# Two layers on one core: reordering dense products, transposes and sums between the hooks of an attention and two feed-forward stages

## The chip, the cores and the metric

The kernel runs on one core of a Trainium2 chip. The metric is the time of one execution in microseconds (us) of device time; lower is better. TensorE is written PE in the profile (PEld is its weight load), VectorE is DVE, ScalarE is ACT, GpSimd is POOL, SyncE is SP.

## The reference

Two layers act on x of 2 x 1024 x 512 in float32. Each takes a layer norm and adds an attention-like branch and a feed-forward branch:

```python
xn = _layernorm(x)
x = x + L0_attn(xn, ...) + L0_ffn(xn, W1, W2, W3)    # scan of rank 8 + small MLP; silu(x W1) * (x W3), Hadamard, W2
xn = _layernorm(x)
x = x + L1_attn(xn, W_qkv, ...) + L1_ffn(xn, w_gate, w_up, w_down)
# L1_attn: 16 heads of 32, causal softmax over 1024 keys, output projection
# L1_ffn: h = silu(xn w_gate) * (xn w_up); keep 2 of every 4 hidden values; h w_down
```

## The kernel before, in words

All matrix products are float32. There are three stages, one after the other.

**Stage a (layer 0).** The hidden width of 2048 is cut into 16 units of `gate_up` (8 for each half of the rows). One unit forms its two products by a scheme with seven half-size products: in order `pa` from `w1`, `pc` from `s[0]`, `pa` from `s[1]`, `pb` (the "other half"), `pa` from `s[2]`, `pa` from `w2`, `pc` from `s[3]`. Each takes TensorE about 3.44 us. `pa`, `pb` and `pc` are pairs of PSUM banks. Between them ScalarE copies `pa` to `e[0..2]` (lines 214, 222, 228) and VectorE adds `pb` or `pc` to an `e` (lines 210, 232, 242); a later product into the same banks waits for that reader. With `split=True`, `pb` is formed in two parts, one before and one after the product from `s[2]`.

At seven places of a unit, `hook(0)` to `hook(6)`, other work is issued. A list holds it: `put0(unit, place, ...)` in stage a, `put1` in stage c; place 8 of unit 2 is hook 1 of unit 3. What is put there:

- The down projection of one pair of units (`down_by_seven`): seven products `m = 0..6` for each of two halves, 1.72 us of TensorE each (line 305). `hidden_first` (lines 273, 274) and `hidden_last` (lines 280, 281) are four VectorE subtractions and additions that make their inputs; product 1 needs the first of `hidden_last`. In stage a `hidden_last` overwrites an input of product 0, so it also waits for that one. `add_u2` (line 323) adds a partial result on GpSimd.
- The low-rank branch, and `prepare_last`, which makes a few small sums with TensorE: four transposes (line 498), three groups of four tiny products (lines 503, 508, 512). The third group needs ScalarE's copy of the transposes.

**Stage b (attention).** There are 8 units `u` (batch and a group of four heads), and 12 steps `(u, j, kt)` for each, 96 in all, numbered `n`. A step issues `weights` (lines 1139, 1145: scores of transposed keys, exp on ScalarE at line 1156, mask at lines 1161 or 1165), then `gather` of the step before (line 1185: weights times values into bank 0; line 1192: sums of the weights), then `maxima` for 13 steps later (line 1082, then VectorE lines 1089, 1090), then one or more **dense parts**: half of a projection (`project`, `values`, `project_out`, line 1030), 1.91 us from start to start of what follows. Dense parts are taken from the list `rest` with entries (earliest step, due step, parts): the ready one with the nearest due step goes first, one part a step, more where the planner (`late`) finds them behind. `put_after(n, ...)` places work right after `gather`; `put(n, ...)` places it at the end of a step. Two such pieces share step 12u+7 and step 12u+15: `total` (line 1204: weight sums to `w`, copied by ScalarE into the single buffer `inv`, then four reciprocals and a product in `divide`) and `shift_rows` (line 1120: transposes of the negated maxima to `px`, copied by VectorE at line 1124).

PSUM in this stage: three pairs of banks, `wide0..2`, are handed out in turn to everything wide: `weights` takes two, `maxima` two, `total` one, `shift_rows` one. Bank 0 holds the output of `gather`. A dense piece takes bank 1 if `alone` is None, and banks 0 and 1 in turn otherwise.

`idle_vector(u, j, kt)` is true from the step on in which no `maxima` are left (`12u + 4j + kt + 13 >= 96`): then masks are made on VectorE, and with `j = 1` the sums of line 1192 too; before that both are GpSimd's.

**Stage c (layer 1 feed-forward)** has 16 units of the same `gate_up`, the same down projection, and between them `sparsify`: one ScalarE and eleven VectorE instructions (lines 1449 to 1464) that keep two of four, issued by `some_steps`. The last pair of units ends in a list `tail`, with whole-row products at line 1508.

Within each stage TensorE, VectorE, ScalarE and GpSimd execute in the order in which the program issues; DMAs on SP are free of it, and so is what comes after the 96 steps.

Of the kernel before, what the change touches and what calls it, by code (L numbers as in the profile page):

```python
# [35 lines left out]
def two_layers(ctx: ExitStack, tc: tile.TileContext, t: dict, out: bass.AP):  # L36
# [315 lines left out]
    with tc.tile_pool(name="a", bufs=1) as a:  # L352
# [131 lines left out]
        def prepare():  # L484
            nc.gpsimd.tensor_mul(gd, gd, factors["dskip"])
            nc.gpsimd.tensor_mul(wo_aug, wo_aug, factors["Wo_by"])
            wa = wp[:, :, R : 2 * R]
            b_wide, wo_t = row("b_wide"), row("wo_t")
            b_wide, wo_t = (v.rearrange("p (k c) -> p k c", c=P) for v in (b_wide, wo_t))
            nc.gpsimd.tensor_copy(b_wide, bcol.unsqueeze(2).to_broadcast([P, KC, P]))  # L490
            ones = a.tile([P, P], F32, name="ones_a")
            nc.gpsimd.memset(ones, 1.0)
            put0(1, 1, prepare_last, wa, b_wide, wo_t, ones)

        def prepare_last(wa, b_wide, wo_t, ones):
            pw, pc = two_banks("prep")
            for k in range(KC):
                nc.tensor.transpose(
                    pw[:, k * P : (k + 1) * P], wo_aug[:, k * P : (k + 1) * P], ident
                )  # L500
            nc.scalar.copy(wo_t.rearrange("p k c -> p (k c)"), pw)
            for k in range(KC):
                nc.tensor.matmul(
                    pc[:, : 2 * R], b_wide[:, k, :], w_io[:, k, :],
                    start=(k == 0), stop=(k == KC - 1),
                )
            for k in range(KC):
                nc.tensor.matmul(
                    pc[:, 2 * R : 3 * R], ones, wa[:, k, :], start=(k == 0), stop=(k == KC - 1)
                )  # L510
            for k in range(KC):
                nc.tensor.matmul(
                    pc[:, 3 * R : 4 * R], wo_t[:, k, :], wa[:, k, :],
                    start=(k == 0), stop=(k == KC - 1),
                )
            nc.vector.tensor_add(c_io, b_io, pc[:, : 2 * R])
            nc.vector.tensor_copy(cs_a, pc[:, 2 * R : 3 * R])
            nc.vector.tensor_copy(woa[:32, :], pc[:32, 3 * R : 4 * R])
# [259 lines left out]
        for n in range(NU - 1):  # L778
            u = 2 * n + 2
            places = [range(7), range(7, 14)]  # L780
            if n == 0:
                places = [(7, 8, 8, 9, 9, 10, 10), (11, 12, 12, 13, 13, 14, 14)]
            elif n == 1:
                places = [range(1, 8), (8, 9, 10, 11, 12, 13, 13)]
            for half, at in enumerate(places):
                put0(u, at[0] - half, hidden_first, n, half)
                for f, *args in products_of(n, half):
                    if f == down:
                        place = at[args[2]]
                    put0(u, place + (f != down), f, *args)  # L790
                    if f == down and args[2] == 0:
                        put0(u, place, hidden_last, n, half)

            for m, (k, f) in enumerate(((1, 1), (3, 1), (6, 1))):
                at = places[1][k] + f
                put0(u, at, down_weights, n + 1, m)
# [142 lines left out]
    with tc.tile_pool(name="b", bufs=1, reuse_waits="tile") as b:  # L939
# [234 lines left out]
        def gather(u, j, kt, s, pts):  # L1174

            bb, hg = units[u]
            if kt == 0:
                held[u, j] = ps_bank(f"o_{u}_{j}", 0)
                sums_of[u, j] = pts
            po = held[u, j]  # L1180
            last = kt == 4 * j + 3
            v = vals[bb, kt // NJ, kt % NJ][:, hg * P : (hg + 1) * P]
            for h in range(4):
                rows = slice(h * HD, (h + 1) * HD)
                nc.tensor.matmul(  # L1185
                    po[rows, s:], v[:, rows], pts[h // 2][:, h % 2, s:],
                    start=(kt == 0), stop=last, tile_position=(0, h * HD),
                )
            if kt:
                eng = nc.vector if j and idle_vector(u, j, kt) else nc.gpsimd  # L1190
                for acc, pt in zip(sums_of[u, j], pts):
                    eng.tensor_add(acc[:, :, s:], acc[:, :, s:], pt[:, :, s:])  # L1192
            if last:
                att[u, j] = b.tile([P, 512], F32, tag="att", name=f"att_{u}_{j}", bufs=12)
                nc.scalar.copy(att[u, j], po)
# [58 lines left out]
        def put_after(n, *what):  # L1254

            after.setdefault(n, []).append(what)

        for u in range(len(units)):

            for half in range(2):  # L1260
                n = per * u - ahead + (3, 11)[half]
                if half:
                    put(n + 1, larger, u)
                for m in range(3):
                    put_mid(n + 2 + m, shift_part, u, half, m)
                put_after(n + 5, shift_rows, u, half)
            if u:
                lo = per * (u - 2) if u > 1 else -ahead
                for x in range(4):
                    rest.append((lo, per * u - ahead - 1, project(u, x // 2, x % 2)))  # L1270
            if u > 1:
                put(per * (u - 2) - 1, load_qk, units[u][1])
            for j in range(2):
                n = per * u + 8 * j + 7
                if n < len(second):
                    put_after(n, total, u, j)
                    for q in range(4):
                        put(n + q * 2 // 3, divide, u, j, q)
                else:
                    put(len(second) + 2, total, u, j)  # L1280
        for x in range(4):
            rest.append((-ahead, x, values(0, 0, x)))
            rest.append((-ahead, 7 + x, values(0, 1, x)))
# [15 lines left out]
        for m in range(QT):  # L1299


            lo, hi = (per * 5 + 6, per * 6 + 3) if m < NJ else (per * 6, per * 8 - 6)
            if m > NJ:
                lo = per * 8 - (17, 14, 2)[m - NJ - 1]
                hi = lo + 1
            rest.append((lo, hi, project_out(m)))

        def do_first(n):
            u, qt, c = first[n]
# [32 lines left out]
        for x in range(4):  # L1342
            for f, *args in project(0, x // 2, x % 2):
                f(*args)
        behind, alone = None, None
        start = mark()
        for n in range(-ahead, len(second)):
            now = weights(*second[n]) if n >= 0 else None
            for f, *args in middle.pop(n, ()):
                f(*args)  # L1350
            if behind is not None:
                gather(*behind)
            behind = now
            for f, *args in after.pop(n, ()):
                f(*args)
            if n < 0:
                one_part(n)
            if n + ahead < len(first):
                do_first(n + ahead)
            if n >= 0 or n % 2:  # L1360
                one_part(n)
            while late(n) and one_part(n):
                pass
            what_is_fixed(n)
# [1 line left out]
        gather(*behind)  # L1366
        alone = 0
        n = len(second)
        for m in range(QT, QT + NJ):
            rest.append((n, n + 9, project_out(m)))  # L1370
        first_tt, *make = combine_x(sums, xt1[0], xt1[1], "c0")
        for m, f in enumerate(make):
            put(n + 5 + m, f)
# [12 lines left out]
    with tc.tile_pool(name="c", bufs=1, reuse_waits="tile") as c_:  # L1386
# [131 lines left out]
        for n in range(groups - 1):  # L1518

            end = n == groups - 2  # L1520
            u = 2 * n + 2
            for half in range(2):
                for at, count in (((0, 2), (1, 5), (2, 5)), ((4, 1), (7, 4), (8, 4), (9, 3)))[half]:
                    put1(u, at, some_steps, n, half, count)
            for last in range(2):
                put1(u - 1, 3 + last, down_weights, n, last)
            for half, at in enumerate(((8, 11),) if end else (range(4, 11), range(11, 18))):
                steps = list(sequence(n, half))
                for place in at:
                    put1(u, place, *steps.pop(0))  # L1530
                    while steps and steps[0][0] != down:
                        put1(u, place + 1, *steps.pop(0))
                tail += steps
            put1(u, 3, hidden_first, n, 0)
            put1(u, 3, hidden_last, n, 0)
            if end:
                put1(u, 3, own_t3, n)
            if not end:
                put1(u, 10, hidden_first, n, 1)
                put1(u, 10, hidden_last, n, 1)  # L1540
# [35 lines left out]
        for n, (pb, g, half) in enumerate(units):  # L1576
# [12 lines left out]
            def hook(at):  # L1589
# [10 lines left out]

            gate_up(
                c_, f"c{n}", gu_w.pop((n, 0)), gu_w.pop((n, 1)), s_of.pop(n), x, y, tt,
                lambda m, i: h[:, 2 * half + m, i, :], hook, split=n < 2 or n == len(units) - 2,
            )
            if n + 2 < len(units):
                load_gu(n + 2)
# [77 lines left out]
```

## Time and profile before

| | |
|---|---|
| time, median of 3 runs | 1833.69 us (1833.6 to 1836.63) |
| the profiled execution's own time | 1834.55 us |
| its span | 1832.8 us, mean granted TensorE clock 0.995 |
| busy: PE, DVE, POOL, ACT | 1795.2, 1126.8, 815.8, 476.8 us |
| stage a, until | 667 us |
| stage b, 667 to 1237 us | 570 us |
| stage c, from | 1237 us |

The profiled execution is one execution; the median comes from others. Views give time in us from the start of the span. In a list of waits, "X <- Y" is X waiting for Y, with the sum, how often, and the longest. In a view by stretches, each engine's busy time stands with its number of instructions, and PEclk is the clock that TensorE was granted (1.00 is full).

### The profile page before, as it was taken

Reading aid. Unit: us, or ns where it says so; the run is one execution under the profiler, and the core shown is the slowest. Engines: PE = TensorE matmul, PEld = TensorE weight load, DVE = VectorE, ACT = ScalarE, POOL = GpSimd, SP = SyncE. Lnnn points to the kernel's source line nnn. Section 1 sums busy time; section 2 is a strip of 40 time slices with the busy share of each in tenths; the row PEclk is TensorE's granted clock in tenths of the full one; section 3 lists DMA queues with packets and bytes.
Section 4 is the critical chain, followed back from the end, with each engine's and each line's share of the span. In section 5 each row is a group of like instructions: output and inputs, shape, how many; then the busy total and the mean of one; then the engine's idle time right before and its main releaser. Section 6 shows DMA issues by size and latency. Waiting matters only on the chain.

```text
span 1832.8 us, 18971 instructions
## 1 busy us (share of the span) xinstructions
PE 1795.2 (98%) x7386; PEld 922.2 (50%) x7386; DVE 1126.8 (61%) x1477; ACT 476.8 (26%) x681; POOL 815.8 (45%) x703
## 2 busy tenths in 40 slices
PE   9999999999999999999999999999999999999999
PEld 5456566555555564333333333334555555555545
DVE  4765544555554348566656566752768778668665
ACT  3222222122211112333343433412212211221220
POOL 5135553354642222467666766713243344244300
PEclk9999999999999999999999999999999999999999
DMA  6121111111110010000001000011011102201101
GB/s 230 46 69 35 46 35 35 35 35 35 35 35 23 12 41 12 1 12 13 13 1 35 12 13 1 24 46 41 29 58 35 46 24 81 80 23 46 46 1 46
DMA packets 29609, 68.12 MB, mean 37 GB/s; under 512 B 3408, under 2 KB 11856, under 8 KB 27984
## 3 DMA queue, kind: packets, MB, share of 16 engines
q1 hardware_dynamic: 28800, 66.61, 11.0%
q8 instruction: 59, 0.97, 0.2%
q10 hardware_dynamic: 720, 0.30, 0.1%
q14 instruction: 30, 0.25, 0.0%
HBM read 62.70 MB, written 4.19 MB: 37 GB/s over the span
## 4 chain that ended last, share of the span: by engine, by line
PE 89%; DVE 6%; POOL 3%; ACT 2%; issue 1%; ACTq 0%; POOLq 0%; DVEq 0%
PE p_a L179 20%; PE p_c L179 20%; PE d L305 19%; PE pq L1030 6%; PE m L1082 4%; PE s L1139 4%; PE o L1185 3%; PE po L1030 3%; PE pv L1030 3%; PE dr L1508 2%; POOL acc L1192 2%; ACT acc L1156 1%; PE w L1204 1%; DVE tops L1090 1%; PE s L1145 1%
## 5 line engine op out<-in xcount | busy, mean ns | idle before, releaser
L323 POOL TENSOR_TENSOR x<-x,de 128x512 f32<-128x512 f32 x87 | 126.1, 1464 | 299.8 <-DVE x L318 163.7
L1192 POOL TENSOR_TENSOR acc<-acc,pt 128x1024 f32<-128x1024 f32 (+3 forms) x144 | 243.3, 1716 | 0.1
L1090 DVE TENSOR_REDUCE tops<-m 128x2 f32<-128x1024 f32 (+2 forms) x192 | 180.8, 956 | 49.1 <-PE m L1082 44.6
L318 DVE TENSOR_TENSOR x<-x,d 128x512 f32<-128x512 f32 x145 | 99.2, 684 | 150.8 <-PE d L305 150.7
L1156 ACT ACTIVATE pt<-s 128x1024 f32<-128x1024 f32 (+3 forms) x160 | 115.4, 766 | 184.4 <-PE s L1145 164.6
L305 PE MATMUL d<-td,h 128*128 128x256 f32 x592 | 141.4, 383 | 4.3 <-DVE h L280 4.3
L305 PEld LDWEIGHTS d<-td,h 128*128 128x128 f32 x592 | 113.2, 192 | 48.7 <-issue 29.2
L1030 PE MATMUL pq<-xt,wqk 128*128 128x512 f32 x256 | 125.1, 617 | 0.8 <-ACT qk L1046 0.8
L179 PE MATMUL p_c<-xt,s_c 128*128 128x512 f32 x256 | 117.7, 603 | 3.7 <-DVE e_c L232 3.7
L179 PE MATMUL p_a<-xt,s_a 128*128 128x512 f32 x256 | 116.6, 598 | 0.9 <-DVE e_a L232 0.9
L179 PE MATMUL p_a<-t_a,s_a 128*128 128x512 f32 x256 | 117.2, 602 | 0.0
L179 PE MATMUL p_a<-xt,w 128*128 128x512 f32 x256 | 115.4, 592 | 0.7 <-ACT xt L136 0.7
L179 PE MATMUL p_c<-xt,gu 128*128 128x512 f32 x256 | 115.8, 592 | 0.0
L1089 DVE TENSOR_TENSOR m<-m,mask 128x256 f32<-128x256 f32 x128 | 54.7, 428 | 97.7 <-PE m L1082 93.2
L179 PE MATMUL p_c<-t_c,s_c 128*128 128x512 f32 x256 | 114.6, 592 | 0.0
L1082 PE MATMUL m<-qk,qk 32*128 32x512 f32 (+3 forms) x768 | 107.7, 535 | 3.6 <-ACT acc L1156 3.0
L1139 PE MATMUL s<-qk,qk 32*128 32x512 f32 (+3 forms) x768 | 93.1, 532 | 3.2 <-ACT pt L1156 2.3
L172 POOL TENSOR_TENSOR s_c<-gu,s_c 128x512 f32<-128x512 f32 x16 | 20.4, 1276 | 142.0 <-PE p_c L179 142.0
L179 PEld LDWEIGHTS p_c<-xt,s_c 128*128 128x128 f32 x256 | 49.5, 194 | 57.1 <-issue 55.9
L1030 PEld LDWEIGHTS pq<-xt,wqk 128*128 128x128 f32 x256 | 44.5, 190 | 66.5 <-issue 62.0
L179 PEld LDWEIGHTS p_a<-xt,s_a 128*128 128x128 f32 x256 | 47.2, 190 | 58.9 <-issue 58.4
L1185 PE MATMUL o<-pt,v 128*32 128x512 f32 (+3 forms) x640 | 70.4, 478 | 5.5 <-DVE pt L1161 4.2
(250 smaller groups left out, 3012.0 us busy)
## 6 DMA issues: line engine op xcount, KB each, us to landing
w<-in_W SPq DMA_DIRECT2D x32, 512.0 KB, 3.6
gu<-in_gu SPq DMA_DIRECT2D x32, 512.0 KB, 3.5
wd<-in_down SPq DMA_DIRECT2D x8, 1024.0 KB, 4.8
x<-in_x SPq DMA_DIRECT2D x16, 256.0 KB, 4.8
w2h<-in_W2q SPq DMA_DIRECT2D x4, 1024.0 KB, 11.4
xr<-in_x SPq DMA_DIRECT2D x16, 256.0 KB, 2.6
wqk<-in_WqkvT SPq DMA_DIRECT2D x16, 256.0 KB, 3.3
out_x<-x SPq DMA_DIRECT2D x15, 256.0 KB, 2.0
```

The source lines that it names most:

```text
L179: nc.tensor.matmul(pair[:, m, :], a[:, m, k, :], x[:, k, :], start=start and k == 0, stop=stop and k == 1, skip_group_check=True,)
L305: nc.tensor.matmul(out_[:, j, :], lhs[:, q, j * P : (j + 1) * P], rhs[:, q], start=m in (0, 1, 3, 4) and j == q == 0, stop=j == q == 1, sk ...
L318: nc.vector.tensor_add(r, r, out_)
L323: nc.gpsimd.tensor_add(r, r, u2[half])
L1030: nc.tensor.matmul(got[0], lhs(k), rhs(k), start=(k == 0), stop=(k == KC - 1))
L1082: nc.tensor.matmul(pair[h // 2][:, h % 2, :e], q[rows, qt * P : (qt + 1) * P], k[rows, c * 512 : c * 512 + e], start=True, stop=True,)
L1089: nc.vector.tensor_add(d, d, mask.unsqueeze(1).to_broadcast([P, 2, P]))
L1090: nc.vector.tensor_reduce(out=tops[u][:, c, qt, 2 * p : 2 * p + 2], in_=pair[p][:, :, :e], axis=mybir.AxisListType.X, op=ALU.max,)
L1139: nc.tensor.matmul(pair[h // 2][:, h % 2, s:], k[rows, kt * P : (kt + 1) * P], q[rows, cols], start=True, stop=False,)
L1156: nc.scalar.activation(pt[:, :, s:], pair[p][:, :, s:], AF.Exp, scale=1.0 / math.sqrt(HD))
L1185: nc.tensor.matmul(po[rows, s:], v[:, rows], pts[h // 2][:, h % 2, s:], start=(kt == 0), stop=last, tile_position=(0, h * HD),)
L1192: eng.tensor_add(acc[:, :, s:], acc[:, :, s:], pt[:, :, s:])
```

## The change

- Stage a: `prepare_last` is split. Transposes and the two groups of sums that need no copy stay at hook 1 of unit 1; the third group and the three VectorE copies go to hook 2.
- Stage a, first down projection (n = 0): its fourteen products move. First half: product 0 stays at hook 0 of unit 3, 1 and 2 go from hook 1 to 2, 3 and 4 from 2 to 3, 5 and 6 from 3 to 4. Second half: 0 and 1 both at hook 5 (before: 4 and 5), 2 and 3 at hook 6 (before 5 and 6), 4, 5 and 6 at hook 0 of unit 4. Its `hidden_first` goes from hook 3 to hook 4.
- Stage b: `shift_rows` is issued ahead of `total` where both share a step. The sums of the last unit's first half, steps (7, 0, 1..3), are VectorE's. In unit 7 the second half's negated maxima (`larger`, `shift_part`, `shift_rows`) are made one step earlier, `total(7, 0)` comes at step 89 instead of 91, and `total(7, 1)` one place earlier.
- Stage b, dense parts: projections of units 3 and later may start a step earlier (steps 11, 23, 35, 47, 59), and their weights are loaded three steps earlier. So steps 11 and 59, which had no dense part, get one. The table below the diff lists the steps. Output projections 5, 6, 7 start at 78, 80 and 82 (before 79, 82, 94), and number 8 starts at 93 (before 96). Before step 0 the dense pieces use banks 0 and 1 in turn.
- Stage c: the first down projection's first half starts one hook later (hook 5 of unit 2); unit 2 is formed with `split=True`; in unit 14 `hidden_first` and `hidden_last` go from hook 3 to hook 6.

```diff
-            put0(1, 1, prepare_last, wa, b_wide, wo_t, ones)
+            banks = []
+            put0(1, 1, prepare_sums, banks, wa, b_wide, wo_t, ones)
+            put0(1, 2, prepare_last, banks, wa, wo_t)
...
             if n == 0:
-                places = [(7, 8, 8, 9, 9, 10, 10), (11, 12, 12, 13, 13, 14, 14)]
+                places = [(7, 9, 9, 10, 10, 11, 11), (12, 12, 13, 13, 14, 14, 14)]
...
-                eng = nc.vector if j and idle_vector(u, j, kt) else nc.gpsimd
+                eng = nc.vector if idle_vector(u, j, kt) else nc.gpsimd
...
+                if half and u == len(units) - 1:
+                    n -= 1
...
-                lo = per * (u - 2) if u > 1 else -ahead
+                lo = per * (u - 2) - 1 if u > 1 else -ahead
...
-                put(per * (u - 2) - 1, load_qk, units[u][1])
+                put(max(per * (u - 2) - 4, -ahead), load_qk, units[u][1])
...
                 n = per * u + 8 * j + 7
+                if (u, j) == (len(units) - 1, 0):
+                    n -= 2
                 if n < len(second):
-                    put_after(n, total, u, j)
+                    sums_at.append((n, total, u, j))
...
-                    put(len(second) + 2, total, u, j)
+                    put(len(second) + 1, total, u, j)
+        for what in sums_at:
+            put_after(*what)
...
-                lo = per * 8 - (17, 14, 2)[m - NJ - 1]
+                lo = per * 8 - (18, 16, 14)[m - NJ - 1]
...
+        for m in range(QT, QT + NJ):
+            lo = len(second) - (3 if m == QT else 0)
+            rest.append((lo, len(second) + 9, project_out(m)))
...
-        behind, alone = None, None
+        behind = None
...
+            if n == 0:
+                alone = None
...
-            for half, at in enumerate(((8, 11),) if end else (range(4, 11), range(11, 18))):
+            for half, at in enumerate(((8, 11),) if end else (range(4 + (n == 0), 11 + (n == 0)), range(11, 18))):
...
-            put1(u, 3, hidden_first, n, 0)
-            put1(u, 3, hidden_last, n, 0)
+            for f in (hidden_first, hidden_last):
+                put1(u, 6 if end else 3, f, n, 0)
...
-                lambda m, i: h[:, 2 * half + m, i, :], hook, split=n < 2 or n == len(units) - 2,
+                lambda m, i: h[:, 2 * half + m, i, :], hook, split=n < 3 or n == len(units) - 2,
```

Working through the planner's list with both sets of entries, the number of dense parts in a step changes so:

| steps | before | after |
|---|---|---|
| -1, 0 | 2, 2 | 3, 1 |
| 11, 59 | 0, 0 | 1, 1 |
| 48 | 2 | 1 |
| 77 | 1 | 0 |
| 78, 81 | 0, 0 | 1, 1 |
| 93, 94, 95 | 0, 1, 1 (output projection 7) | 1, 1, 0 (output projection 8) |
| after step 95, before `total` of the last half | 3 | 2 |

## The prediction

> **What bounds the kernel now.** I read the page first: TensorE (PE) is busy nearly all of the span, and 89% of the chain that ended last is PE's. So only three things can shorten it: PE's own gaps (1832.8 - 1795.2 = 37.6 us, of which some 8 are start and end), PE work that runs slower than it could, and a clock below full.
>
> ```profile
> span 1832.8 us, 18971 instructions
> PE 1795.2 (98%) x7386; PEld 922.2 (50%) x7386; DVE 1126.8 (61%) x1477; ACT 476.8 (26%) x681; POOL 815.8 (45%) x703
> PE 89%; DVE 6%; POOL 3%; ACT 2%; issue 1%; ACTq 0%; POOLq 0%; DVEq 0%
> ```
>
> Then the waits of PE alone, which name the places of the gaps:
>
> ```profile
> PE d L305 <- DVE h L280: 4.3, 4, 2.5
> PE o L1185 <- DVE pt L1161: 4.2, 5, 1.6
> PE p_c L179 <- DVE e_c L232: 3.7, 1, 3.7
> PE w L1204 <- DVE tops L1090: 2.9, 6, 0.5
> PE s L1139 <- ACT pt L1156: 2.3, 3, 1.0
> PE d L305 <- DVE h L1464: 1.8, 2, 1.5
> ```
>
> Third, stretches of 3.41 us around these places, for the granted clock (PEclk):
>
> ```profile
> 60.00:63.41 3.41, 3.41 (x24) 2.82 (x24) 3.38 (x3) 0.40 (x1) 0.74 (x1) 1.00 0.25 80
> 63.41:66.82 3.41, 3.41 (x5) 1.35 (x4) 3.41 (x7) 0.00 (x0) 0.00 (x0) 0.50 0.24 73
> 121.44:124.85 3.41, 1.38 (x4) 0.31 (x2) 3.27 (x3) 0.00 (x0) 3.41 (x3) 1.00 0.00 0
> 124.85:128.26 3.41, 2.98 (x7) 2.44 (x8) 2.02 (x2) 0.00 (x0) 1.50 (x1) 0.50 0.00 0
> 1046.45:1049.86 3.41, 3.36 (x18) 1.64 (x19) 1.12 (x3) 2.25 (x4) 3.41 (x5) 0.50 0.00 0
> 1302.45:1305.86 3.41, 1.90 (x8) 1.44 (x8) 3.38 (x4) 0.86 (x3) 0.45 (x1) 1.00 0.00 0
> 1742.77:1749.59 6.82, 5.14 (x6) 2.19 (x7) 3.42 (x5) 1.12 (x2) 0.00 (x0) 0.50 0.00 0
> ```
>
> Half clock holds for 17.1 us in all and costs half of that, 8.5 us (the mean clock of 0.995 says the same). It comes in pieces of 3.41 us, each after a stretch with little PE work: 1.38 busy of 3.41, or (60.00) tiny products. The limit isn't sharp: after 1.90 busy (1302.45) the clock stays, before 1046.45 there were 2.15 busy, of products that fill a quarter of the rows.
>
> Last, the timeline where `total` and `shift_rows` meet (columns: start, length, engine, line):
>
> ```profile
> 812.54 1.06 PE L1204 MATMUL w<-acc,ones 128*32 128x512 f32 x8 [0.48 <-DVE tops L1090]
> 813.53 0.40 PE L1120 MATMUL px<-identb,parts 128*128 128x128 bf16 x4
> 813.66 0.59 ACT L1209 COPY inv<-w 128x512 f32<-128x512 f32 x1 [1.50 <-PE w L1204]
> 813.86 1.56 PE L1082 MATMUL m<-qk,qk 32*128 32x512 f32 x8
> 815.36 1.98 PE L1030 MATMUL pq<-xt,wqk 128*128 128x512 f32 x4
> ```
>
> **The change part by part.** Gains are positive; the sum is made against the profiled execution (1834.55 us).
>
> *A, small sums split.* In 60.00-63.41 tiny products fill 2.2 us up to 62.16. After, the third group (0.9 us) runs 3.44 us later, so 1.24 us of them stay there. No work is saved; the half clock (1.7 us) should go. 0 to 1.7; I take 1.2, since the 3.41 us pieces may lie otherwise.
>
> *B, first down projection in stage a.* PE waits 2.47 us at 122.82 for VectorE's L280 (with the lost overlap 2.63), then runs at half clock (1.7); 0.24 at 154.08 (0.4 with overlap). After, a product of 3.44 us lies ahead of product 1 of the first half, so that wait goes: 4.7 back in all. But products 0 and 1 of the second half now share a hook with `hidden_last` between them: product 1 waits for L280, which waits for product 0. This pattern stands at the end of stage a, where each such wait is 0.84 and 0.79 (1.0 with overlap) at L280 of 0.69; beside GpSimd's sums L280 took 1.57 to 1.76, so up to 1.9. Take 1.4. What queues behind it on VectorE (L281, the sums of product 1) has 3.44 us of cover. Net 3.3 (2.5 to 3.7).
>
> *C, two banks before step 0.* PE waits of 0.78 at 685.12, 0.27 at 707.23, 0.53 at 724.91, each for the reader of bank 1. All go: 1.6 (1.4 to 2.0). The extra dense part before step 0 is moved work.
>
> *D, transposes ahead of sums.* In such a step `weights` has pairs x and y, `w` gets z, `px` gets x, and `maxima` y and z. z is free only when ScalarE has copied `w` (0.59 after both exps), so `maxima` start half: 1.50 us from 813.86 to 815.36, where with `px` alone (753.27) they take 1.07. After, z is `px`'s, and VectorE's copy (0.42, it starts as `px` ends, VectorE idle) is over while `w` (0.97) still runs. 0.43 for each of the 13 steps 7 to 79 that have both and `maxima`: 5.6. The 0.48 that `w` waits in six of them becomes `px`'s, since it comes from z's former reader, VectorE. 0 to 5.6; take 5.6.
>
> *E, steps 11 and 59.* At 795.54 and 1043.77 PE waits 1.03 and 1.02 for an exp that waited for GpSimd's sums, then 0.25 for a mask. A dense part (1.91) there leaves 0.47 of its length uncovered by wait: 1.44 each, 2.9. With step 59's half clock (1.7): 4.6 (2.5 to 4.6). Weights arrive in 3.3 us and have three steps of 5 us, SP is not late.
>
> *F, steps 77 to 83.* Steps 78 and 81 lack a dense part; the following scores wait for pairs: 0.9 and 1.4 over their normal 1.29 and 0.8. Now only 77 lacks one, about 0.95. Gain 1.4 (0.5 to 2).
>
> *G, last unit.* Six sums (2 x 0.95, 2 x 0.69, 2 x 0.42 = 4.1 us by VectorE's rows) move to it. For this the four masks before, 5.56 us for four beside GpSimd's sums against 0.42 alone, get about 4 us shorter. `total` at 89 brings four reciprocals (3.76) ahead of the crowded steps 92 to 95; but `inv` is one buffer: ScalarE's copy must wait until GpSimd's product for unit 6 has read it. Between the two copies lie sums (2 x 0.69, 2 x 0.42) and four reciprocals on VectorE and GpSimd's 1.27, 7.2 us, against 4.8 us of PE's (scores 2 x 1.29, products 0.36 and 0.88, `w` 0.97): a wait of some 2.4, and the next exps queue behind it. From 1180.34 to 1208.24 VectorE is busy 25.4 of 27.9 us, so it bounds this end, and its work is the same. 0 (-2 to +3).
>
> *H, after step 95.* The wait of 0.59 for bank 1 goes. The last `total` is covered by four dense parts (6.9 us) against its chain of 6.2 us (1214.58 to 1220.78): 0.6. If that cover failed, the excess would show whole.
>
> *I, unit 2 of stage c.* At 1301.54 and 1302.53 PE waits 0.29 and 1.51 (2.1 with overlap) for `sparsify`. After, product 0 comes 3.44 us later and does not wait. But then the `pc` product stands next, and it needs L232, which VectorE reaches behind L1464, L210 and `hidden_first/last`, at 1309.0 in the trace; PE would be there at 1306.5: a new wait of 2.5. Net -0.4, and a half-clock stretch is likely (six in ten, 1.7): -1.4 (-2.2 to +1).
>
> *J, unit 14.* There the very same wait costs 3.71 at 1740.74 and two half-clock stretches. VectorE's row:
>
> ```profile
> 1740.31 0.68 DVE L273 TENSOR_TENSOR sd<-h 128x512 f32<-128x512 f32 x1
> 1743.09 1.21 DVE L232 TENSOR_TENSOR e_c<-e_c,p_c 128x1024 f32<-128x1024 f32 x1
> 1744.45 6.22 PE L179 MATMUL p_c<-xt,s_c 128*128 128x512 f32 x8 [3.71 <-DVE e_c L232]
> ```
>
> Without L273 to L281 ahead of it L232 starts 2.8 us earlier: the wait shrinks to 0.9, and the clock stays (3.4): 6.2 (4.5 to 6.3). Moved behind L242 these four delay only `sparsify`, whose next user is 10 us off.
>
> Sum: 1.2 + 3.3 + 1.6 + 5.6 + 4.6 + 1.4 + 0 + 0.6 - 1.4 + 6.2 = 23.1 us; 1834.55 - 23.1 = 1811.4. The profiled execution lies 0.9 above the median, so I forecast 1811.0 for the median.
>
> A rule to weigh: the Trainium skill, "TensorE: Matmul & The Clock Gate", section "Why this matters for your kernels", asks only for "No PE-idle gaps >~3µs between matmul bursts". By it only J's gap would have cost clock, and A, B and E would bring 1.2, 1.7 and 1.7 less, I 1.0 more: 19.5 us, 1815 for the profiled execution. The trace has half clock after gaps of 2.47 and 1.02 and after none at all (63.41), so I keep the trace.
>
> **The rivals.**
>
> *Clock and swap give little.* If the new small waits (B, I, G) fall so that half-clock pieces stay about as many (A, B, E, a part of J), 6 us are lost; or if `maxima` in D wait for something else, 5.6. For it: such pieces need not lie alike in two kernels; runs of one kernel differ by 3 us. Against: the big gaps go. 1811 + 6 = 1817.
>
> *Slower: VectorE takes over the end of attention.* In steps 86 to 95 sums, masks and eight reciprocals queue on VectorE, `inv` holds ScalarE, PE starves and drops to half clock. The price is the growth of a stretch that is 27.9 us now. To outweigh the other gains (23 us) it must reach some 51 us; were it doubled, the time would be 1811 + 28 = 1839. Against: VectorE's work there stays within 2 us of before, and masks lose GpSimd's contention.
>
> *Nothing happens.* If PE's idle were spread by some other limit (gaps that reopen one hook later, as in I), 1833. Against: PE is the bound in 98% of the span, and I, G are the only places where I find a wait that takes over.
>
> **How the numbers follow.** 0.2% (3.7 us) is about what a measurement can tell from no change. Likeliest case 1806-1816: 0.60. Clock or swap lost, 1816-1826: 0.24. More than counted (G at its best, no new waits), below 1806: 0.10. No change: 0.02. Slower: 0.04. Faster is 0.60 + 0.24 + 0.10 = 0.94. The range 1804 to 1822 leaves out slower, none, the far part of the second case and a little below.
>
> **What would show it.** PE's busy time falls by some 12 us and its gaps by as much. `w` and `px` swapped, `maxima` after them 1.07 instead of 1.50 (D). No wait at steps 11 and 59. No 3.71 wait in unit 14, full clock there (J). A new wait of about 2.5 for L232 in unit 2 of stage c (I), one of 0.8 to 1.9 for L280 in unit 3 of stage a (B). ScalarE's copy to `inv` at step 89 waits for GpSimd (G). I am wrong if `maxima` stay at 1.50, if half-clock time stays near 17 us, or if the stretch of the last unit grows beyond 40 us.

## The result and the profile after

The kernel after takes 1816.92 us (median of five runs, 1816.24 to 1819.67) against 1833.69 for the kernel before (1832.77 to 1836.63): a ratio of 0.9906, 95% interval 0.9891 to 0.992, or 16.8 us less. The forecast was 1811.0, with a range of 1804 to 1822: the direction and the range hold, the gain is 5.9 us smaller than the 22.7 forecast. The profiled execution takes 1816.24, its span is 1814.5. Line numbers of the kernel after are 6 higher in stage b than before (`total` L1210, `shift_rows` L1126, `maxima` L1088).

The page of the kernel after:

```profile
span 1814.5 us, 18967 instructions
PE 1784.9 (98%) x7386; PEld 915.2 (50%) x7386; DVE 1140.8 (63%) x1483; ACT 476.5 (26%) x681; POOL 806.5 (44%) x697
PE 92%; DVE 5%; ACT 1%; issue 1%; POOL 0%; POOLq 0%; DVEq 0%; ACTq 0%
```

PE still sets the end. Its busy time fell by 10.3 us and its gaps by 8.0 (1832.8 - 1795.2 = 37.6 before, 1814.5 - 1784.9 = 29.6 now), where the forecast named some 12 and as much. PE's waits in the kernel after:

```profile
PE d L305 <- DVE h L280: 4.9, 3, 3.3
PE p_c L179 <- DVE e_c L232: 3.4, 2, 2.5
PE px L1126 <- DVE tops L1096: 3.4, 7, 0.5
PE m L1088 <- ACT acc L1162: 3.0, 8, 0.7
PE w L1210 <- DVE neg L1130: 1.5, 1, 1.5
PE o L1191 <- DVE pt L1167: 1.4, 2, 1.1
```

Set against the waits of before: the 3.7 for L232 (unit 14) has shrunk to 0.9, but a 2.5 for the same line has come in unit 2 of stage c; L280 costs more than before (4.9 against 4.3), with one place of 3.3; the waits for the exps (`s` for `pt`, 2.3) and for the thinned rows L1464 (1.8) are gone; the 0.5 before the sums is now before `px`. Two stretches of 3.41 us at the ends of the two large waits (columns as before the change: PE busy first, PEclk third from the end):

```profile
151.16:154.57 3.41, 3.12 (x8) 2.52 (x9) 0.92 (x2) 0.00 (x0) 0.00 (x0) 0.58 0.00 0
1293.40:1296.80 3.40, 0.99 (x3) 0.54 (x4) 3.27 (x5) 1.92 (x4) 0.00 (x0) 1.00 0.26 101
```

Behind the 3.27 wait of stage a the clock is halved (from 151.71 on), behind the 2.48 of stage c it is not, in this execution. That piece of 3.41 us is the only half clock before the last microsecond, where the kernel before had 17.1 us of it.

### The profile page after: what moved, and what is told of

Read it like the earlier page. It is cut to its first block, busy times and chain, and to the rows that moved or that the text cites. A ratio compares the mean times of both kernels' runs of the same rounds, so it can differ in the third digit from the quotient of the medians.

```text
span 1814.5 us, 18967 instructions
## 1 busy us (share of the span) xinstructions
PE 1784.9 (98%) x7386; PEld 915.2 (50%) x7386; DVE 1140.8 (63%) x1483; ACT 476.5 (26%) x681; POOL 806.5 (44%) x697
## 4 chain that ended last, share of the span: by engine, by line
PE 92%; DVE 5%; ACT 1%; issue 1%; POOL 0%; POOLq 0%; DVEq 0%; ACTq 0%
PE p_a L179 21%; PE p_c L179 20%; PE d L305 19%; PE pq L1036 6%; PE m L1088 5%; PE s L1145 4%; PE o L1191 3%; PE pv L1036 3%; PE po L1036 3%; PE dr L1526 2%; ACT acc L1162 1%; PE s L1151 1%; PE w L1210 1%; PE pp L603 1%; PE pw L439 1%
## 5 line engine op out<-in xcount | busy, mean ns | idle before, releaser
L1198 POOL TENSOR_TENSOR acc<-acc,pt 128x1024 f32<-128x1024 f32 (+3 forms) x138 | 233.8, 1717 | 0.0
L1088 PE MATMUL m<-qk,qk 32*128 32x512 f32 (+3 forms) x768 | 102.8, 533 | 3.9 <-ACT acc L1162 3.0
L1088 PEld LDWEIGHTS m<-qk,qk 32*128 32x128 f32 x768 | 39.8, 183 | 72.7 <-issue 24.8
```

What stands on the lines that cost most here:

```text
L1088: nc.tensor.matmul(pair[h // 2][:, h % 2, :e], q[rows, qt * P : (qt + 1) * P], k[rows, c * 512 : c * 512 + e], start=True, stop=True,)
```

## The experiments

Ratios are to the kernel before, run on the same chip. A local "lead" is the difference between two traces of the time at which the same product starts; it shows an edit of 0.3 us that the medians do not, but it is read from one execution of each kernel. A "piece" is a stretch of 3.41 us at half clock.

**The first down projection of stage a, undone (B).**

```diff
-                places = [(7, 9, 9, 10, 10, 11, 11), (12, 12, 13, 13, 14, 14, 14)]
+                places = [(7, 8, 8, 9, 9, 10, 10), (11, 12, 12, 13, 13, 14, 14)]
```

> The kernel after, with the places of the first down projection of stage a (n = 0) put back to those before. Forecast's theory (term B): the new places bring 3.3 us net, so this kernel takes 1816.9 + 3.3 = 1820.2. Theory from the profile after: the new places only moved the wait (from 2.47 us at 122.82 to 3.27 us at 148.18, each followed by one 3.41 us piece at half clock), worth about -0.5, so this kernel takes 1816.4, its wait for L280 at about 121 is 2.5 again with half clock behind it, and the 3.27 at 148 is gone.

Measured: 1817.43, ratio 0.9913 (0.9899 to 0.9926), not to be told from the kernel after by the medians. In the traces this kernel is 0.25 us ahead of the kernel after once both have passed unit 4 of stage a, each with one half-clock piece there. So B brought -0.25 and not +3.3: the wait moved within unit 3, from hook 1 (first half) to hook 5 (second half).

**The same, mended.**

```diff
-                places = [(7, 9, 9, 10, 10, 11, 11), (12, 12, 13, 13, 14, 14, 14)]
+                places = [(7, 9, 9, 10, 10, 11, 11), (12, 13, 13, 13, 14, 14, 14)]
```

> The kernel after, with product 1 of the second half one hook later (places 12, 13, 13, 13, 14, 14, 14). Theory: product 1 stood at 148.18 in the same hook as hidden_last, which queues on VectorE behind the statistics of branch_add; one hook later VectorE is done, so the 3.27 wait (3.44 with its overlap) and the half-clock piece behind it (1.7) go: 1816.9 - 5.1 = 1811.8. Rival: three products in one hook wait for VectorE's reads of their banks (up to 1.5 each), and 1814 or more is left. A second rival: the half clock comes from the products' pattern and not from the wait; then it stays, 1813.5.

Measured: 1814.03, ratio 0.9894 (0.988 to 0.9907). PE's waits of this kernel:

```profile
PE d L305 <- DVE h L280: 1.6, 2, 0.8
PE d L305 <- DVE de L315: 0.5, 1, 0.5
```

The 3.3 is gone; what is left of L280 is the old pair at the end of stage a (0.84 and 0.79). Three products in a hook bring one wait of 0.48 for L315, where the rival had up to 1.5. The lead at this place is 4.4 us: 2.8 of wait and 1.6 of half clock. The median is only 2.9 below that of the kernel after, with intervals that overlap; the profiled execution has half clock elsewhere instead (6.83 us at 23.62, 3.41 at 1293), so that the 1.6 need not show in a median.

**The swap alone, on the kernel before (D).**

```diff
+        sums_at = []
...
-                    put_after(n, total, u, j)
+                    sums_at.append((n, total, u, j))
...
+        for what in sums_at:
+            put_after(*what)
```

> The kernel before, with the totals put behind the shift rows within a step (the swap D) and nothing else. Forecast: 13 steps of 0.43 each, 5.6 us: 1828.1. Profile after: maxima behind both take 1.07 as forecast, but the step gets only 0.44 where the 0.48 wait was absent and 0.30 where it was there, since products and sums drain longer; 13 steps give 4.4 to 4.8: 1829.1. Rival (maxima wait for something else): 1833.7.

Measured: 1829.74, ratio 0.9978 (0.9969 to 0.9986): 4.0 us, 2.6 to 5.7. Step by step the lead rises by 0.29 seven times and by 0.44 six times, 4.67 up to step 80, and then falls by 0.8 at step 88: the scores take a bank that VectorE's copy of `px` must have read, this copy stands behind 4.85 us of masks in VectorE's queue, and the group of scores takes 2.56 us where it took 1.75.

**Unit 14 alone, on the kernel before (J).**

```diff
-            put1(u, 3, hidden_first, n, 0)
-            put1(u, 3, hidden_last, n, 0)
+            for f in (hidden_first, hidden_last):
+                put1(u, 6 if end else 3, f, n, 0)
```

> The kernel before, with hidden_first and hidden_last of the last unit but one of stage c (unit 14) at hook 6 instead of 3, and nothing else. Forecast (term J): 2.8 us of wait and 3.4 us of half clock, 6.2: 1827.5. Profile after: the lead gained there is 5.3, since the waiting inside the half-clock pieces had been counted twice: 1828.4. Rival: the half clock there has another cause and stays; 2.8 only, 1830.9.

Measured: 1829.52, ratio 0.9976 (0.9966 to 0.9985): 4.4 us, 2.7 to 6.2. The local lead is 5.33: the wait goes from 3.71 to 0.93 (2.8), and the 6.83 us of half clock behind it are gone (2.5).

**Steps 11 and 59, undone (E).**

```diff
-                lo = per * (u - 2) - 1 if u > 1 else -ahead
+                lo = per * (u - 2) if u > 1 else -ahead
...
-                put(max(per * (u - 2) - 4, -ahead), load_qk, units[u][1])
+                put(per * (u - 2) - 1, load_qk, units[u][1])
```

> The kernel after, with the dense parts' earliest step and the load of their weights put back (so steps 11 and 59 have no dense part again). Forecast (term E): the parts bring 2.9 us without and 4.6 with the half clock at step 59, so this kernel takes 1820 to 1821.5. Theory from the profile after: the wait of 1.03 and the mask's 0.25 are filled, but the maxima of the step behind then wait for their bank until ScalarE's first exp is done (1.45 instead of 0.68), which gives 0.77 back at each place; net 0.9 to 1.0 each: 1816.9 + 1.9 = 1818.8, with waits of 1.0 at steps 11 and 59 and maxima of 0.68 at steps 12 and 60. The half clock at step 59 may be there or not (theory: pieces fall by the phase of a 3.41 us grid and differ between executions of one kernel); with it 1.7 more in that execution.

Measured: 1818.78, ratio 0.9918 (0.9903 to 0.9933). The expected 1818.8 was met by luck: the medians do not tell this kernel from the kernel after, and in the traces the two differ by only 0.7 us without clock and without the odd rows of VectorE told of at the end, not by the 1.9 expected. A dense part takes 1.91 us; at steps 11 and 59 it costs 0.90 and 0.82, so about 1.0 of it lies in the wait. But without E the planner puts the second part at step 78, where it costs 0.97 and hides as much. The two profiles have 3.41 us (after) and 6.83 us (this kernel) of half clock, none of it at step 59.

What took back the rest at steps 11 and 59 is seen in the kernel after, in the step that follows:

```profile
793.67 1.14 PE L1145 MATMUL s<-qk,qk 32*128 32x512 f32 x8
795.05 1.94 ACT L1162 ACTIVATE acc<-s 128x1024 f32<-128x1024 f32 x2 [2.34 <-PE s L1151]
795.32 1.52 PE L1088 MATMUL m<-qk,qk 32*128 32x256 f32 x8
796.13 0.30 PEld L1088 LDWEIGHTS m<-qk,qk 32*128 32x128 f32 x4 [0.52 <-ACT acc L1162]
```

The scores no longer wait, but the `maxima` behind them take a bank pair that the first exp must have read: the second four products start only at 796.13, and the group takes 1.45 us from start to next where it took 0.68 before. No gap over 0.12 shows it, since half of the products fill it.

**Unit 2 of stage c, mended (I).**

```diff
-                put1(u, 6 if end else 3, f, n, 0)
+                put1(u, 6 if end else 3 + (n == 0), f, n, 0)
```

> The kernel after, with hidden_first and hidden_last of unit 2 of stage c (n = 0) at hook 4 instead of 3. Theory: L232 and up(0, 0) then stand ahead of L273 to L281 on VectorE, as in unit 14, and the wait of 2.48 at 1293.33 goes: 1816.9 - 2.5 = 1814.4, or 1813.5 on the mean over executions, since a half-clock piece that stands behind this wait in some of them goes too. Rival: the four operations then delay the products of the hidden rows and PE waits a hook later (as this change itself did here): 1816 or more.

Measured: 1814.65, ratio 0.9893 (0.9879 to 0.9908). The wait of 2.48 is gone (the lead there is 2.72), and nothing opens behind it. The same cause and the same cure as in unit 14.

**Sums of the last unit back on GpSimd (G).**

```diff
-                eng = nc.vector if idle_vector(u, j, kt) else nc.gpsimd
+                eng = nc.vector if j and idle_vector(u, j, kt) else nc.gpsimd
```

> The kernel after, with the row sums of the last unit's first half (u = 7, j = 0) back on GpSimd. Forecast (term G): 0, between -2 and +3. Theory from the profile after: these sums on VectorE make the negated maxima's copy late (a wait of 1.50 before the weight sums at 1169.65), but on GpSimd they would hold the masks and the first exps as before; the stretch of steps 84 to 95 stays within 1 us: 1816.9, from 1815.9 to 1817.9. Rival: VectorE is the bound of this stretch, and taking 4 us from it wins 2 or more: 1815 or less.

Measured: 1817.49, ratio 0.9911 (0.9894 to 0.9928), the same as the kernel after. The wait of 1.50 before `w` is gone, and steps 84 to 95 still take 0.6 us longer, with one half-clock piece in them that the kernel after does not have. Whether VectorE or GpSimd does these sums, the stretch does not change by more than a microsecond or so.

**Two banks alone, on the kernel before (C).**

```diff
+            if n == 0:
+                alone = None
             now = weights(*second[n]) if n >= 0 else None
```

> The kernel before, with dense parts on two banks before step 0 (term C) and nothing else. Forecast: the waits of 0.78, 0.27 and 0.53 at 685, 707 and 725 go, 1.6 us up to step 0. Profile after: 2.3 up to step 0 with the extra dense part taken out; so either the waits cost more than their gaps show (2.3 here too), or the extra dense part before step 0 lies in a wait of its own (1.6 here).

One execution, 1829.96. The lead grows by 2.30 up to step 0, in four jumps: 1.05 at 685, 0.34 at 707, 0.31 at 719 and 0.60 at 725. The first, second and fourth are the forecast's waits of 0.78, 0.27 and 0.53 plus 0.07 to 0.27 of lost overlap; at 719 no gap of 0.2 us is seen. The extra dense part is not the reason, for here there is none.

**Both kernels once more, unchanged.**

> The kernel before, unchanged, profiled once more. Forecast's theory: half clock follows a stretch with little PE work, so it is found again behind 60 to 63 us, behind the wait at 122.8, behind step 59 and in unit 14, 17.1 us in all. Rival: where a piece falls depends on how a 3.41 us grid lies over the stretch in that execution; then at least one of the first three is missing or there is one elsewhere, the waits of PE being the same to 0.1 us, and only unit 14 (3.71 us of wait) has it for certain.

> The kernel after, unchanged, profiled once more. Forecast's theory: half clock behind the wait at 148.18 alone, full clock at 1293. Rival (grid): a piece may stand behind the 2.48 wait at 1293 or elsewhere this time, and VectorE's larger (L1106), 4.6 us in units 3 to 5 in the first trace, takes 0.7 in some of them; spans of the two traces differ by 1 to 3 us.

The kernel before, second execution: 1835.53. Its waits of PE behind the first 10 us are those of the first, to 0.1 us:

```profile
PE d L305 <- DVE h L280: 4.3, 4, 2.5
PE o L1185 <- DVE pt L1161: 4.2, 5, 1.6
PE p_c L179 <- DVE e_c L232: 3.7, 1, 3.7
```

and its half clock lies elsewhere. The stretches at the small sums, behind the wait of 2.47 and behind step 59, which all had 0.50 in the first execution, and then step 11 and unit 14:

```profile
63.20:66.60 3.40, 3.40 (x25) 2.92 (x25) 3.37 (x3) 0.51 (x1) 0.85 (x1) 1.00 0.27 77
126.05:129.46 3.41, 2.55 (x12) 2.27 (x13) 2.89 (x3) 0.00 (x0) 1.93 (x2) 1.00 0.00 0
1049.00:1052.40 3.40, 3.40 (x24) 1.51 (x28) 2.16 (x4) 1.78 (x4) 3.40 (x6) 1.00 0.00 0
798.49:801.90 3.41, 3.41 (x18) 1.66 (x19) 1.51 (x4) 2.14 (x4) 3.41 (x6) 0.50 0.00 0
1743.98:1750.81 6.83, 5.61 (x7) 2.52 (x8) 2.97 (x4) 1.11 (x2) 0.00 (x0) 0.50 0.00 0
```

Only unit 14 is as it was. There are 6.83 us more at 23.66, so the total is the same 17.1 us by chance. The kernel after, second execution: 1819.39, with 13.65 us of half clock (at 24.5, 154.2, 1171.4 and 1297.7) where the first had 3.41; the wait of 2.48 in stage c has half clock behind it this time:

```profile
1297.68:1301.09 3.41, 3.41 (x5) 1.33 (x4) 1.33 (x3) 1.06 (x3) 0.00 (x0) 0.50 0.02 5
```

**Both mends together.** The edits of the two mended kernels above, in one.

> The kernel after with both mends: product 1 of the second half in unit 3 of stage a one hook later, and hidden_first and hidden_last of unit 2 of stage c at hook 4. Each alone took about 2.9 and 2.3 us off; no instruction of the one is near the other, so both together 5.2: 1816.9 - 5.2 = 1811.7, with no PE wait over 1.6 us in the trace. Rival: the half-clock pieces move to other places and take some of it back: 1813.5.

Measured: 1810.16 (1808.04 to 1811.02), ratio 0.9867 (0.9851 to 0.9884). The interval does not touch that of the kernel after, and 1833.69 x (0.9906 - 0.9867) is 7.2 us less than it: about as much as the two leads together, 4.4 and 2.7, and more than the 5.2 expected from the medians. No wait of PE is over 1.51 us. One half-clock piece stands at 24.6 and one in the last unit of stage b (1161.2).

## Why the forecast was right, and where its terms failed

The forecast was right in what bounds the kernel (PE, through its gaps) and in most of the waits that it named, and its range held. Of the 23.1 us of its terms 16.8 came: 1.7 is missing outside the clock and 3.9 in it, as worked out below, and 0.7 is left open by the medians. That the part outside the clock comes out so close owes something to luck, since B and D fell short by 2.8 us while C and E to H gave 1.1 more than forecast. (The terms as they stand give 1834.55 - 23.1 - 0.9 = 1810.6; the forecast wrote 1811.0.)

Traces of the same kernel differ in their half-clock pieces, so the sum is kept here in two columns: what the terms said without clock, and what the traces show without it.

| term | forecast, no clock | shown, no clock | by |
|---|---|---|---|
| A small sums | 0 | 0 | traces |
| B first down projection | 1.6 | -0.25 | undone |
| C two banks | 1.6 | 2.3 | alone |
| D swap | 5.6 | 4.7 | alone, up to step 80 |
| E to H, steps 11, 59 and 77 on | 4.9 | 5.3 | what the others leave of 14.4 |
| I unit 2 | -0.4 | -0.4 | traces |
| J unit 14 | 2.8 | 2.8 | alone |
| sum | 16.1 | 14.4 | |

The 14.4 is the difference of the two profiled spans, 18.3, less the clock that the two pay in them (7.0 before: 1.70, 1.45, 1.32 and 2.55; 1.6 after), and with 1.5 us added back for three odd rows of VectorE told of below: 18.3 - 7.0 + 1.6 + 1.5.

*A.* No work is saved, as forecast. The half clock at 63.41 was there in one of five profiles of kernels that leave the sums whole, so the split is worth some 0.3 on the mean, not 1.2.

*B.* The failing step is the size of the new wait, "up to 1.9. Take 1.4". It was taken from L280's own duration. The queue of VectorE in the kernel after shows what stood ahead of it:

```profile
146.63 0.68 DVE L666 BATCH_NORM_STATS2 sty<-y 128x6 f32<-128x512 f32 x1
147.44 0.66 DVE L666 BATCH_NORM_STATS2 sty<-y 128x6 f32<-128x512 f32 x1
148.24 1.49 DVE L200 TENSOR_TENSOR h<-h,e_a 128x512 f32<-128x512 f32 x1
149.65 1.74 DVE L280 TENSOR_TENSOR h<-h 128x512 f32<-128x512 f32 x1
151.44 1.42 PE L305 MATMUL d<-td,h 128*128 128x256 f32 x3 [3.27 <-DVE h L280]
```

Product 0 is done at 148.18, and L280 waits for it. VectorE is then just ending the statistics of `branch_add` and has L200 before L280: L280 starts 1.47 us late, at 149.65. Then it is slow itself, 1.74 beside GpSimd's L171 (L281 behind it takes 0.69). Together that is the wait of 3.27 instead of 1.4. The forecast looked at what queues behind L280 and not at what is ahead of it.

*C.* The mechanism was right; the waits cost 0.07 to 0.27 more than their gaps, and there were four and not three.

*D.* The `maxima` behave as forecast, 1.07 instead of 1.50, and `neg` is copied while `w` runs:

```profile
809.64 0.38 PE L1126 MATMUL px<-identb,parts 128*128 128x128 bf16 x4 [0.48 <-DVE tops L1096]
809.96 1.06 PE L1210 MATMUL w<-acc,ones 128*32 128x512 f32 x8
810.07 0.42 DVE L1130 COPY neg<-px 128x512 bf16<-128x512 bf16 x1 [0.57 <-PE px L1126]
810.95 1.14 PE L1088 MATMUL m<-qk,qk 32*128 32x512 f32 x8
```

The term that was too large is "0.43 for each of the 13 steps": in the seven that had no wait of 0.48, the group of `o` ahead of `px` now takes 0.12 longer from its start to the next (1.00 for 0.88) and `w` 0.03 longer, so that only 0.29 is won; and 0.8 is lost at step 88 when the swap stands alone, where VectorE is still at masks as `px` ends and not idle, as the term has it.

*E.* The term of 2.9 left out what comes late next: the `maxima` of the following step, 0.77 us each time. (Its 1.44 for a place is also 0.16 more than the two waits that it names, 1.03 and 0.25.) The direct gain is some 1.0 at each place, and against a kernel without E it is 0.7 in all, since one of the two parts hides as much at step 78.

*F to H.* F's wait of the scores (0.9) and the 0.6 of `o` behind it are gone, and no gap over 0.2 is left between 1124 and 1164. The group E to H comes out 0.4 above its sum, but that is a remainder and proves nothing. A lead splits it once: at step 88 the kernel after is 8.19 us ahead and has done two dense parts more (3.82); less the 3.48 of lead before step 0, D's 4.67 and step 59's 1.32 of clock, and with the odd rows' 1.5, this is 4.0 for E, F and the last unit's first steps (4.3 forecast for E and F), and 1.3 is left for what follows (0.6). F and H were not run by themselves, so their sizes stay open. G is 0 as forecast. ScalarE's copy to `inv` does wait for GpSimd's product, but 0.60 and not 2.4:

```profile
1177.09 1.28 POOL L1222 TENSOR_TENSOR att<-att,inv 128x512 f32<-128x512 f32 x1 [11.55 <-DVE inv L1220]
1178.40 0.59 ACT L1215 COPY inv<-w 128x512 f32<-128x512 f32 x1 [0.60 <-POOL att L1222]
```

The slower rival, a stretch of 28 us growing to more than 50, is refuted: from step 88 to the last `w` it takes 33.2 us before (1180.34 to 1213.59) and 28.9 after (1172.15 to 1201.07); 3.4 of that difference is PE work that now stands elsewhere (PE is busy 30.1 of it before and 26.7 after).

*I and J.* The same queue, once cured and once made. Unit 14 in the kernel after, and unit 2 of stage c:

```profile
1727.33 1.20 DVE L232 TENSOR_TENSOR e_c<-e_c,p_c 128x1024 f32<-128x1024 f32 x1
1728.68 1.52 PE L179 MATMUL p_c<-xt,s_c 128*128 128x512 f32 x3 [0.92 <-DVE e_c L232]
```

```profile
1291.68 0.68 DVE L273 TENSOR_TENSOR sd<-h 128x512 f32<-128x512 f32 x1
1293.84 0.69 DVE L281 TENSOR_TENSOR sd<-h,sd 128x512 f32<-128x512 f32 x1
1294.45 1.21 DVE L232 TENSOR_TENSOR e_c<-e_c,p_c 128x1024 f32<-128x1024 f32 x1
1295.81 2.38 PE L179 MATMUL p_c<-xt,s_c 128*128 128x512 f32 x5 [2.48 <-DVE e_c L232]
```

Forecast 0.9 and 2.5, measured 0.92 and 2.48: these two orders within one queue were priced to 0.1 us from the rows of before, because all that stands ahead in it was counted. J's clock was not: half of 6.83 us was booked, 3.4, though PE was busy for only 5.14 of them, and 2.5 came.

*The clock* is where most of the missing gain went. The forecast gave 8.0 us to clock (A, B, E, J) and took 1.0 for I, 7.0 net, by pinning each piece of one execution to its stretch. The trace of one execution cannot say what another will do. Twenty runs of the kernel before, made together on one chip, go from 1829.25 us at a mean clock of 0.999 to 1836.31 at 0.994, with a correlation of -0.98 and 1.55 us for each 0.001. Their mean clock is 0.996, that of the five runs of the kernel after 0.998: the clock saved some 3.1 us, not 7.0, and 16.8 - 3.1 = 13.7 is close to the 14.4 of the traces. J is the one place where the piece is certain. The Trainium skill, "TensorE: Matmul & The Clock Gate", section "Why this matters for your kernels", warns of gaps over about 3 us, and the forecast set it aside for the trace; the profiles put both in their place:

| gap of PE ahead | half clock behind it |
|---|---|
| 3.71 (unit 14) | 4 of 4 profiles, two pieces each |
| 3.27 (stage a, after) | 4 of 5 |
| 2.47 (stage a, before) | 3 of 6 |
| 2.48 (unit 2 of stage c, after) | 4 of 6 |
| 1.51 (unit 2 of stage c, before) | 1 of 5 |
| 1.02 (step 59), 1.03 (step 11) | 2 of 6, 1 of 6 |
| 1.51 and 1.35 (before `w` and `o` of the last unit, after) | 1 of 7, 2 of 2 |
| 1.32 and 1.60 (end of stage b, before) | 0 of 5 each |
| none (small sums whole) | 1 of 5 |

Above 3 us it is nearly sure, which the section says; below it is not excluded, only less likely, which it leaves out. By the section alone the profiled execution would have been 1815, by the forecast 1811.4; it was 1816.24.

The thirteen traces also show what decides. In each of them every half-clock piece starts a whole number of times 3.413 us after the first full clock: in the first trace of the kernel before that is at 5.38, and the pieces at 63.41, 124.85, 1046.45 and 1742.77 stand 17, 35, 305 and 509 steps behind it. This grid lies differently in each execution (first full clock from 4.36 to 7.48). Whether a piece follows goes by PE's busy time in the one stretch of the grid before it, so the same wait counts when it falls into one stretch and not when the grid cuts it in two:

| wait, with full-size products around it | PE busy in the 3.41 us ahead, half clock followed | not followed |
|---|---|---|
| 2.47 (stage a, before) | 0.94, 1.17, 1.38 | 1.50, 1.74, 1.79 |
| 3.27 (stage a, after) | 0.27, 0.65, 0.89, 1.10 | 1.82, then 1.74 |
| 2.48 (unit 2 of stage c, after) | 0.93 four times | 1.56, 1.86 |
| 3.71 (unit 14, before) | 0.70, 0.93, 1.07, 1.39 | |
| 1.51 (unit 2 of stage c, before) | 1.61 | 1.91, 2.15, 2.28, 2.51 |

No stretch under 1.49 us of PE work was followed by full clock in any of the traces. In stage b, where many products fill a quarter of the rows (steps 11 and 59, the last unit), busy time alone does not part the cases: a piece followed 1.91 to 2.16 us there in six stretches, and others as busy had none. At the small sums it followed 3.41 us of tiny products. An estimate from these figures: if more than 1.9 us idle in a stretch bring the piece, and a wait of w falls anywhere in the grid, it comes in (3.41 + w - 3.8) / 3.41 of the executions, which is 0.61 for 2.47, 0.84 for 3.27 and 0.97 for 3.71; seen were 7 of 12 (2.47 and 2.48), 4 of 5 and 4 of 4. It misses the one piece behind 1.51, after 1.80 of idle time.

## What to carry to other kernels

Price a moved instruction by everything that stands ahead of it in its queue at its new place, not by its own duration: that is the difference between B (1.4 forecast, 3.27 measured) and I (2.5 and 2.48). When a stall is filled, follow the released step one stage on, to the next bank that it takes; a lost overlap shows as a longer group and not as a gap. Never book a half-clock piece of one execution at its full price: take the mean clock of many runs, or a second profile of the same kernel, and a chance for each gap that grows with its length; a piece also costs only about half of what PE is busy in it (unit 14: 2.5 for 6.83 us).

## What the runs showed that was not expected

The position of half clock differs between executions of one kernel with identical waits, and so does the time, by 7 us in 1830. At 23 to 25 us, behind the start, seven of the thirteen profiles have one or two such pieces and six none. The traces part them by the grid alone: first full clock at 4.36 to 5.94 us, no piece; at 6.31 to 6.59, two; at 7.22 to 7.48, one. What stands there from 19.7 us on is 32 products of 24 columns (L597 before, L603 after) with eight transposes between, so PE is busy for 3.21 of the 3.41 us ahead of the piece; as at the small sums, the clock fell behind tiny products though PE was busy. Other work at this place was not tried.

VectorE's `larger` (L1106 after, 128 x 16 elements) took 4.62 us in units 3, 4 and 5 of the first trace of the kernel after, 0.72 in the second:

```profile
915.73 4.62 DVE L1106 TENSOR_TENSOR tops<-tops 128x16 f32<-128x16 f32 x1
```

```profile
917.41 0.72 DVE L1106 TENSOR_TENSOR tops<-tops 128x16 f32<-128x16 f32 x1
```

Its order in VectorE's queue is the same in both, and GpSimd's sums and masks run beside it both times. In the second it ends at 918.13, as the sum that GpSimd was at does (914.52 + 3.58 = 918.10). In the first it ends at 920.35, after that sum, two masks, two more sums and two more masks (919.54 + 0.78 = 920.32). The Trainium skill, "SBUF — State Buffer", section "Who interferes with whom", says that a VectorE instruction with two SBUF inputs contends with a GpSimd instruction that reads SBUF, and that the second to come is blocked until the first is done; the second trace agrees, the first has the instruction last over several of GpSimd's. Each long one made the following scores 0.5 to 0.6 us later. It came in other units of other kernels too (3.7 us in units 2 to 4 and 4.6 in unit 5 of the kernel with unit 14 alone, none in the swap alone), so it belongs to an execution and not to this change. What decides it was not tried.
